# Layer-1 attention: row blocks' softmax sums inverted in pairs instead of one by one

## The chip, the cores and the metric

One Trainium2 chip, of which the program uses one core. The metric is the device time of one execution in microseconds, the median of three runs. TensorE is PE (its weight loads PEld), VectorE is DVE, ScalarE is ACT, GpSimd is POOL, and SyncE is SP.

## The reference, cut to what matters

Two layers. Each normalises `x`, and adds an attention and a feed-forward part to it. The change touches the attention of layer 1, a causal one with 32 query heads over 8 shared key/value heads of 128 elements, on 2 batches of 1024 rows with 512 features.

```python
# layer 1, attention
q = (hidden_states @ Wq.T)                     # 32 heads of 128
k, v = ...                                     # 8 heads of 128, through a low-rank latent
k = jnp.repeat(k, n_rep, axis=1)               # n_rep = 4
v = jnp.repeat(v, n_rep, axis=1)
scores = jnp.einsum('bhqd,bhkd->bhqk', q, k) * scale
scores = jnp.where(causal, scores, -1e9)
attn = jax.nn.softmax(scores, axis=-1)
out = jnp.einsum('bhqk,bhkd->bhqd', attn, v)
...
return out @ Wo.T
```

Layer 0 has a non-causal attention with one head of 128 and a branch with 50 Sinkhorn iterations; layer 1 also has a gated LoRA feed-forward (FFN).

## The kernel before

**Precision.** All matmuls work on float16. A float32 operand is held as a high part (its float16 rounding) and a low part (what is left, again in float16), and a product is made of three passes, high x high, high x low and low x high (`mm3`, L89).

**Row blocks.** Layer 1 runs over 16 groups (2 batches x 8 key/value heads, `g`), each with 32 row steps (`s`). A row step takes 32 query positions of the group's four heads, 128 rows in all, against the first W = 32(s+1) keys, since the attention is causal. It is traced by `row_step`, called at L868:

- `rows_scores`: the scores, by three matmuls into a PSUM bank of tag `s`, or six into two banks when W is over 512. There are four such banks (BS).
- `rows_exp`: on DVE, scale, mask and copy of the scores into `P`, with a running extremum into `nm` (L284 for the masked piece, L288 for the other); then on ACT `P = exp(P)` with the row's sum into `r[:, 0:1]` (L292).
- `rows_hi`: on DVE the reciprocal of the sum (L316), on ACT its scaling by 16384 (L317) and the high part of `P * r` into `Phl` (L322).
- `rows_lo`: on DVE the low part (L330; two pieces where a block's last key tile is mixed, in groups 8 to 15), on POOL a memset of the padding (L334), and on SP a DMA transpose of `Phl` into `PT` (L335).

`row_step` runs one step behind with the last two: step s traces the scores of block s, then `rows_hi` of block s-1, `rows_exp` of block s, and `rows_lo` of block s-1. The list `pending` holds at most one block.

**Buffers.** `P` has three buffers (PB) and `Phl` three (LB). A buffer holds four blocks for s below 8, two for s from 8 to 15, and one from 16 on (`share`). `nm` and `r` have four, `PT` three.

**Fillings.** After each row step of layer 1 come the pieces of other work that are due there (`fill`): the AV matmuls of a pair of blocks (`av`, L365), due in step 4c+2k+5 for blocks 4c+2k and 4c+2k+1, the evacuation of their result into `ao` (L105, L106), the output projection (`wo_block`, L755), the next group's query, key and value projections, the fetching of weights and their splitting on POOL (`parts_of`), and for part of the run the Sinkhorn iterations, the second layer norm, the gating and the FFN of the batches. Some of these are ordered behind the low part traced last (`last_low`).

**Order.** The order of tracing is a priority. The program is built with a planner (`schedule_with_timeline_sim=True`) that sets each engine's order of instructions by its own model of time, keeping dependencies, buffers and the orderings written out with `behind` and `issue_after`. So an engine's order in the profile differs from the order of tracing, and the score matmuls of two row steps often stand next to each other.

Layer 0 uses the same `row_step`, from L480, for 16 blocks of W = 1024, and flushes it with a `row_step()` without arguments (L483). Layer 1 does so once, after its last step.

Of the kernel before, what the change touches and what calls it, by code (L numbers as in the profile page):

```python
# [11 lines left out]
AF = mybir.ActivationFunctionType  # L12
# [4 lines left out]
P = 128  # L17
# [12 lines left out]
QR = 32  # L30
# [14 lines left out]
MG = range(8, 16)  # L45
# [3 lines left out]
PSCALE = 16384.0  # L49
# [3 lines left out]
def tile_model(ctx: ExitStack, tc: tile.TileContext, out: bass.AP, a: dict):  # L53
# [3 lines left out]
    V, A, G = nc.vector, nc.scalar, nc.gpsimd  # L57
# [7 lines left out]
    def T(tag, shape, dt=F32, bufs=None):  # L65
        count[0] += 1
        kw = {} if bufs is None else {"bufs": bufs}
        return sb.tile(shape, dt, tag=tag, name=f"{tag}_{count[0]}", **kw)
# [115 lines left out]
    last_hi, last_lo, last_low = [None], [None], [None]  # L184
# [82 lines left out]
    def share(got, n, k, make):  # L267

        if k % n == 0:
            got[0] = make()  # L270
        return got[0][:, k % n]

    P_of, hl_of = [None], [None]

    def rows_exp(pieces, causal, scale, n, k):

        W = pieces[-1][0] + pieces[-1][1]
        Pm = share(P_of, n, k, lambda: T("P", [P, n, S // n], bufs=PB))
        nm = T("nm", [P, 2], bufs=4)
        last = None  # L280
        for k, (o, w, pt) in enumerate(pieces):
            first = 1.0e30 if last is None else last
            if causal and o + w == W:
                last_row[0] = V.tensor_tensor_reduce(Pm[:, o:o + w], pt[:, :w], mask[:, 512 - w:],  # L284
                                       -scale, first, ALU.add, ALU.min,
                                       nm[:, k:k + 1])
            else:
                last_row[0] = V.tensor_scalar(Pm[:, o:o + w], pt[:, :w], -scale, first,  # L288
                                ALU.mult, ALU.min, accum_out=nm[:, k:k + 1])
            last = nm[:, k:k + 1]  # L290
        r = T("r", [P, 2], bufs=4)
        A.activation(Pm[:, :W], Pm[:, :W], AF.Exp, bias=last, scale=-1.0,  # L292
                     accum_out=r[:, 0:1])
        return Pm, r, W

    def rows_parts(W, n, k, mix=False):

# [14 lines left out]
        v = hl.rearrange("p (l k) -> p l k", l=2)  # L312
        return hl, v[:, 0, :W], [(0, W, v[:, 1, :W])], v[:, :, W:] if W < m * P else None

    def rows_hi(Pm, r, W, pool, hl):
        V.reciprocal(r[:, 1:2], r[:, 0:1])  # L316
        A.activation(r[:, 1:2], r[:, 1:2], AF.Copy, scale=PSCALE)  # L317
        if pool:
            A.activation(Pm[:, :W], Pm[:, :W], AF.Copy, scale=r[:, 1:2])
            A.activation(hl[1], Pm[:, :W], AF.Copy)  # L320
        else:
            A.activation(hl[1], Pm[:, :W], AF.Copy, scale=r[:, 1:2])  # L322

    def rows_lo(Pm, r, W, pool, hl, dst):
        whole, hi, los, pad = hl
        for a0, a1, lo in los:
            if pool:
                G.tensor_tensor(lo, Pm[:, a0:a1], hi[:, a0:a1], ALU.subtract)
            else:
                last_low[0] = V.scalar_tensor_tensor(lo, Pm[:, a0:a1], r[:, 1:2], hi[:, a0:a1],  # L330
                                                     ALU.mult, ALU.subtract)
        if pad is not None:

            behind(G.memset(pad, 0.0), last_low[0])  # L334
        nc.sync.dma_start_transpose(dst[:, :whole.shape[1] // P], whole)  # L335

    pending = []

    def row_step(q=None, K=None, W=None, causal=None, scale=None, dst=None, pool=None, n=1, k=0,
                 mix=False):  # L340

        if q is not None:
            pieces = rows_scores(q, K, W)
        old = None
        if pending:
            old = pending.pop()
            rows_hi(*old[:5])
        if q is not None:
            pending.append((*rows_exp(pieces, causal, scale, n, k), pool, rows_parts(W, n, k, mix), dst))
        if old:  # L350
            rows_lo(*old)

    def out_tile():
        count[0] += 1
# [311 lines left out]
    SC1 = 1.0 / (math.sqrt(128.0) * 128.0)  # L666
# [108 lines left out]
    def fetch_q(g, hh):  # L775
        qw[g, hh] = fetch(a["Wq"][4 * (g % NG) + hh])
# [8 lines left out]
    def layer1_attn(kv0, start, extra):  # L785


        N, NS = NB * NG, S // QR
        fill = {}

        def at(g, s, f):
            g, s = g + s // NS, s % NS
            fill.setdefault((g, s), []).append(f)

        kvs, Qs, PTs, avs, aos, wos = [{} for _ in range(6)]

        def twice(g):
            Vm = kvs[g]["Vm"] = [T("xr", [P, NT, P], F16, bufs=XB) for l in range(2)]
            for l in range(2):
                for k in range(2):  # L800
                    nc.sync.dma_start(Vm[l][64 * k:64 * k + 64], kvs[g]["V"][0:64, l])

        def q_unit(g, u):
            half, hh = divmod(u, 4)
            if hh == 0:
                Qs[g, half] = T("Q", [P, 2, NS // 2, 4, QR], F16, bufs=2)
            qproj(g // NG, qw[g, hh], Qs[g, half], hh, half)

        def fetch_wo(g, hh):
            n = 4 * (g % NG) + hh  # L810
            wos[g, hh] = fetch(a["WoT"][n * P:(n + 1) * P, :])

        def split_wo(g, hh):
            wos[g, hh] = parts_of(wos[g, hh], "wo", 32.0, WB)

        def av(g, c, k):
            if k == 0:
                avs[g, c] = out_tile()
            aos[g, c] = group_av(kvs[g]["V"], kvs[g].get("Vm"), PTs[g, 2 * c + k], c, k, avs[g, c])

        def wo(g, c):
            wo_block(g // NG, c, aos[g, c], [wos[g, h] for h in range(4)], g % NG == NG - 1)

        kvs[0], fs = kv0
        start(fs[2:], lambda u: q_unit(0, u))
        for hh in range(4):
            fetch_wo(0, hh)
            split_wo(0, hh)
        for g in range(N):
            if g + 1 < N:  # L830
                new = (g + 1) % NG == 0
                kvs[g + 1], fs = kv((g + 1) // NG, (g + 1) % NG)
                at(g, KVN - 2 if new else 1, fs[0])
                for k, f in enumerate(fs[1:]):
                    at(g, KVN + 2 * k if new else 1 + 4 * k + 2 * (k == 0), f)
                for hh in range(4):
                    at(g, 5 + 4 * hh, lambda g=g, hh=hh: fetch_q(g + 1, hh))
                    at(g, 7 + 4 * hh, lambda g=g, hh=hh: split_q(g + 1, hh))
                for u in range(4):
                    at(g, QNN + 2 * u if new else QN + 4 * u, lambda g=g, u=u: q_unit(g + 1, u))  # L840
                for hh in range(4):
                    s = 26 + 2 * hh if new else 22 + 3 * hh
                    at(g, s - 2, lambda g=g, hh=hh: fetch_wo(g + 1, hh))
                    at(g, s, lambda g=g, hh=hh: split_wo(g + 1, hh))
            for u in range(4):
                at(g, QH + (1 if (g + 1) % NG == 0 else 3) * u, lambda g=g, u=u: q_unit(g, 4 + u))
            if g in MG:
                at(g, 2, lambda g=g: twice(g))
            for c in range(NT):
                for k in range(2):  # L850
                    at(g, 4 * c + 2 * k + AVD, lambda g=g, c=c, k=k: av(g, c, k))
                at(g, 4 * c + WOD, lambda g=g, c=c: wo(g, c))
        for k, fs in extra.items():
            fill[k] = fs + fill.get(k, [])
        for g in range(N + 1):
            for s in range(NS):
                if g < N:
                    c, r = divmod(s, NR)

                    n = 4 if c < 2 else 2 if c < 4 else 1  # L860
                    if c < 4 and r == 0:
                        PT = T("PT", [P, 2 * (c + 1), NR, P], F16, bufs=3)
                        for k in range(2):
                            PTs[g, 2 * c + k] = PT[:, :, 2 * k:2 * k + 2]
                    elif c >= 4 and r % 2 == 0:
                        PTs[g, s // 2] = T("PT", [P, 2 * (c + 1), 2, P], F16, bufs=3)
                    Qt, q0 = Qs[g, s // (NS // 2)], s % (NS // 2)
                    row_step(lambda l: Qt[:, l, q0].rearrange("p h q -> p (h q)"),  # L868
                             kvs[g]["K"], QR * (s + 1), True, SC1, PTs[g, s // 2][:, :, r % 2], False, n, r, g in MG)
                elif pending:  # L870
                    row_step()
                for f in fill.pop((g, s), []):
                    f()
        assert not fill, sorted(fill)
# [131 lines left out]
    PTs = attn0_rows(0, 0, *f0[0][:2], lambda: adv(CA))  # L1006
    ys0 = branch0(0, *f0[0][3:5], lambda: adv(CB))
    attn0_out(0, 0, f0[0][2], PTs)
    PTs = attn0_rows(0, 1, *f0[0][:2], lambda: adv(CA))
# [6 lines left out]
    for half in range(2):  # L1016
# [5 lines left out]
        PTs = attn0_rows(1, half, *f0[1][:2], lambda: adv(CD))  # L1022
# [153 lines left out]
```

## Time and profile before

| | |
|---|---|
| median of 3 runs | 1848.31 us (1847.91 to 1849.43) |
| span of the profiled execution | 1846.2 us |
| PE busy, share of the span | 93% |
| DVE busy, share of the span | 80% |
| ACT busy, share of the span | 65% |
| L292 exponential, ACT, 528 of them | 391.5 us, mean 742 ns |
| L322 high part, ACT, 515 | 369.5 us, mean 730 ns |
| L330 low part, DVE, 627 | 460.8 us, mean 759 ns |
| L335 transpose, issue to landing, median | 3.2 us |

The span is the time from the first to the last instruction of one execution under the profiler. Busy time of an engine leaves out its waits. Matmuls are pipelined and their ends are modelled, so that a busy PE is not in itself a PE at its peak; the spacing of their starts tells more. Of a wait for several semaphores the last is named.

### The profile page before, as it was taken

How to read it: one execution, taken by the hardware profiler on the slowest of the kernel's cores; microseconds unless marked ns; L12 is line 12 of the kernel's file. 1: busy time of each engine (PE TensorE's matmuls, PEld its weight loads, DVE VectorE, ACT ScalarE, POOL GpSimd, SP SyncE). 2: the span in 40 equal slices, each digit the busy share in tenths (PEclk: the TensorE clock that was granted, in tenths of full speed). 3: DMA queues.
4: the chain of work that ended last, by engine and by line, in shares of the span. 5: the costliest groups of instructions: out<-in, count | busy, mean ns of one | idle time of the engine just before them, and what ended most of it. 6: DMA issues, size and time to landing. Idle time of an engine off the chain costs nothing.

```text
span 1846.2 us, 35059 instructions
## 1 busy us (share of the span) xinstructions
PE 1708.2 (93%) x11394; PEld 1038.5 (56%) x11394; DVE 1473.1 (80%) x4162; ACT 1191.1 (65%) x2917; POOL 896.5 (49%) x1476
## 2 busy tenths in 40 slices
PE   4666389999999999998999999999999999999998
PEld 2434146566666566655555566666666666666565
DVE  8888968988888878778976768778787877787675
ACT  4848666656676778876544656667666767676564
POOL 5568629778766465647634433323242424235200
PEclk9888699999999999999999999999999999999999
DMA  7435225656575656468645656556566655566455
GB/s 212 82 56 132 59 44 123 151 118 139 119 149 98 141 128 144 105 142 143 146 98 125 144 126 140 135 124 141 125 134 124 142 118 142 124 143 135 97 121 118
DMA packets 693482, 230.25 MB, mean 125 GB/s; under 512 B 674081, under 2 KB 674209, under 8 KB 693298
## 3 DMA queue, kind: packets, MB, share of 16 engines
q1 hardware_dynamic: 677842, 180.75, 47.3%
q0 software_dynamic: 13152, 43.07, 8.7%
q10 hardware_dynamic: 2304, 4.20, 0.7%
q8 instruction: 89, 1.46, 0.3%
q14 instruction: 95, 0.78, 0.1%
HBM read 52.81 MB, written 4.19 MB: 31 GB/s over the span
## 4 chain that ended last, share of the span: by engine, by line
PE 47%; DVE 2%; DMA 1%; POOL 1%; issue 1%; ACT 0%; SPq 0%; DVEq 0%
PE pp L89 26%; PE av L365 11%; PE s L89 10%; DVE Phl L330 0%; DVE f2k L913 0%; DMA f2k<-in_Wq 0%; DMA xT<-wo 0%; DVE P L288 0%; POOL wo L241 0%; DMA PT<-Phl 0%; POOL f2k L95 0%; SPq L335 0%; DVE P L284 0%; DMA twT<-twhl 0%; DVE Q L106 0%
## 5 line engine op out<-in xcount | busy, mean ns | idle before, releaser
L292 ACT ACTIVATE P<-P,nm 128x1024 f32<-128x1024 f32 (+31 forms) x528 | 391.5, 742 | 280.9 <-DVE nm L284 263.4
L330 DVE SCALAR_TENSOR_TENSOR Phl<-P,r,Phl 128x64 f16<-128x64 f32 (+16 forms) x627 | 460.8, 759 | 75.7 <-ACT Phl L322 70.3
L89 PE MATMUL s<-K,Q 128*128 128x512 f16 (+22 forms) x2400 | 439.1, 317 | 19.7 <-DVE P L288 11.7
L365 PE MATMUL av<-PT,V 128*128 128x256 f16 x3456 | 425.6, 274 | 9.4 <-DMA PT<-Phl 8.5
L365 PEld LDWEIGHTS <-V 128*128 128x128 f16 x3456 | 338.2, 98 | 92.9 <-DMA PT<-Phl 10.6
L322 ACT ACTIVATE Phl<-P,r 128x1024 f16<-128x1024 f32 (+31 forms) x515 | 369.5, 730 | 20.6 <-DMA PT<-Phl 5.3
L89 PE MATMUL pp<-xT,wq 128*128 128x512 f16 x1536 | 371.8, 381 | 4.5 <-DVE Q L106 2.3
L89 PE MATMUL pp<-wo,ao 128*128 128x512 f16 x1536 | 369.9, 379 | 2.0 <-ACT ao L105 1.9
L95 POOL TENSOR_SCALAR f2k<-f2k 128x512 f32<-128x512 f32 x164 | 113.9, 695 | 500.6 <-DVE Phl L330 458.9
L89 PEld LDWEIGHTS <-Q 128*128 128x128 f16 x2400 | 222.8, 98 | 175.7 <-issue 27.7
L89 PEld LDWEIGHTS <-wq 128*128 128x128 f16 x1536 | 149.7, 98 | 172.6 <-issue 6.8
L89 PEld LDWEIGHTS <-ao 128*128 128x128 f16 x1536 | 149.5, 98 | 156.9 <-ACT ao L105 3.4
L284 DVE CUSTOM_DVE_ANT_0 P<-s,mask,nm 128x272 f32<-128x272 f32 (+15 forms) x256 | 157.3, 615 | 9.3 <-PE s L89 1.0
L288 DVE TENSOR_SCALAR_CACHE_REDUCE P<-s 128x512 f32<-128x512 f32 (+15 forms) x272 | 152.6, 562 | 13.4 <-PE s L89 11.2
L316 DVE RECIPROCAL r<-r 128x1 f32<-128x1 f32 x528 | 78.9, 154 | 87.5 <-ACT P L292 84.5
L317 ACT ACTIVATE r<-r 128x1 f32<-128x1 f32 x528 | 95.6, 192 | 60.2 <-DVE r L316 59.7
L105 ACT ACTIVATE ao<-av 128x512 f16<-128x512 f32 x128 | 74.9, 585 | 81.7 <-PE av L365 81.5
L334 POOL MEMSET Phl<- 128x192 f16 (+1 forms) x320 | 56.2, 189 | 142.3 <-DMA PT<-Phl 97.3
L105 ACT ACTIVATE Q<-pp 128x512 f16<-128x512 f32 x128 | 74.6, 583 | 64.3 <-PE pp L89 60.0
L284 DVE CUSTOM_DVE_ANT_0 P<-s,mask 128x32 f32<-128x32 f32 (+15 forms) x256 | 103.7, 430 | 14.9 <-PE s L89 14.2
L755 DVE SCALAR_TENSOR_TENSOR acc<-pp,acc 128x512 f32<-128x512 f32 x128 | 87.1, 681 | 35.1 <-PE pp L89 34.7
L106 DVE SCALAR_TENSOR_TENSOR Q<-pp,Q 128x512 f16<-128x512 f32 x128 | 87.4, 683 | 34.0 <-ACT Q L105 33.7
(256 smaller groups left out, 2153.1 us busy)
## 6 DMA issues: line engine op xcount, KB each, us to landing
f2k<-in_Wq POOLq DMA_DIRECT2D x64, 256.0 KB, 3.1
f2k<-in_WoT POOLq DMA_DIRECT2D x64, 256.0 KB, 3.3
PT<-Phl SPq DMA_TRANSPOSE x528, 3.2
acc<-in_x SPq DMA_DIRECT2D x16, 256.0 KB, 5.1
f2k<-in_Wup POOLq DMA_DIRECT2D x16, 256.0 KB, 3.3
out<-acc ACTq DMA_DIRECT2D x16, 256.0 KB, 3.5
xr<-V SPq DMA_DIRECT2D x32, 128.0 KB, 2.4
xr<-in_x SPq DMA_DIRECT2D x12, 256.0 KB, 3.9
```

The lines of the kernel that those rows point to most:

```text
L89: nc.tensor.matmul(dst, lhs(l), rhs(r), start=(i == 0 and j == 0), stop=(i == n - 1 and j == 2))
L95: first = G.tensor_scalar(stage, stage, scale, 1.0, ALU.mult, ALU.mult)
L105: A.activation(hl_hi, src, AF.Copy, scale=scale)
L106: return V.scalar_tensor_tensor(hl_lo, src, scale, hl_hi, ALU.mult, ALU.subtract)
L284: last_row[0] = V.tensor_tensor_reduce(Pm[:, o:o + w], pt[:, :w], mask[:, 512 - w:], -scale, first, ALU.add, ALU.min, nm[:, k:k + 1])
L288: last_row[0] = V.tensor_scalar(Pm[:, o:o + w], pt[:, :w], -scale, first, ALU.mult, ALU.min, accum_out=nm[:, k:k + 1])
L292: A.activation(Pm[:, :W], Pm[:, :W], AF.Exp, bias=last, scale=-1.0, accum_out=r[:, 0:1])
L317: A.activation(r[:, 1:2], r[:, 1:2], AF.Copy, scale=PSCALE)
L322: A.activation(hl[1], Pm[:, :W], AF.Copy, scale=r[:, 1:2])
L330: last_low[0] = V.scalar_tensor_tensor(lo, Pm[:, a0:a1], r[:, 1:2], hi[:, a0:a1], ALU.mult, ALU.subtract)
L365: nc.tensor.matmul(p, v, pt, start=(k == 0), stop=(k == len(todo) - 1))
L755: V.scalar_tensor_tensor(acc[b, t], p, 1.0 / 256.0, acc[b, t], ALU.mult, ALU.add)
```

## The change

In layer 1 a tile `r` holds the sums of two row blocks and their inverses, four columns in place of two. The even block's exponential opens it and writes its sum to column 0, the odd block's writes to column 1. `pending` gathers blocks until both are there. The next even row step then makes one reciprocal and one scaling for both (`rows_inverse`), the high parts of both blocks before its own exponential, and the low parts, memsets and transposes of both after it. An odd row step traces only its scores and its exponential. Layer 0 keeps one block at a time (`rows=1`), with the same instructions as before.

```diff
--- before.py
+++ after.py
@@ -272,7 +272,7 @@
 
     P_of, hl_of = [None], [None]
 
-    def rows_exp(pieces, causal, scale, n, k):
+    def rows_exp(pieces, causal, scale, n, k, total):
 
         W = pieces[-1][0] + pieces[-1][1]
         Pm = share(P_of, n, k, lambda: T("P", [P, n, S // n], bufs=PB))
@@ -288,10 +288,9 @@
                 last_row[0] = V.tensor_scalar(Pm[:, o:o + w], pt[:, :w], -scale, first,
                                 ALU.mult, ALU.min, accum_out=nm[:, k:k + 1])
             last = nm[:, k:k + 1]
-        r = T("r", [P, 2], bufs=4)
         A.activation(Pm[:, :W], Pm[:, :W], AF.Exp, bias=last, scale=-1.0,
-                     accum_out=r[:, 0:1])
-        return Pm, r, W
+                     accum_out=total)
+        return Pm, W
 
     def rows_parts(W, n, k, mix=False):
 
@@ -312,43 +311,52 @@
         v = hl.rearrange("p (l k) -> p l k", l=2)
         return hl, v[:, 0, :W], [(0, W, v[:, 1, :W])], v[:, :, W:] if W < m * P else None
 
-    def rows_hi(Pm, r, W, pool, hl):
-        V.reciprocal(r[:, 1:2], r[:, 0:1])
-        A.activation(r[:, 1:2], r[:, 1:2], AF.Copy, scale=PSCALE)
+    def rows_inverse(r):
+        n = r.shape[1] // 2
+        V.reciprocal(r[:, n:], r[:, :n])
+        A.activation(r[:, n:], r[:, n:], AF.Copy, scale=PSCALE)
+
+    def rows_hi(Pm, W, inv, pool, hl):
         if pool:
-            A.activation(Pm[:, :W], Pm[:, :W], AF.Copy, scale=r[:, 1:2])
+            A.activation(Pm[:, :W], Pm[:, :W], AF.Copy, scale=inv)
             A.activation(hl[1], Pm[:, :W], AF.Copy)
         else:
-            A.activation(hl[1], Pm[:, :W], AF.Copy, scale=r[:, 1:2])
-
-    def rows_lo(Pm, r, W, pool, hl, dst):
+            A.activation(hl[1], Pm[:, :W], AF.Copy, scale=inv)
+
+    def rows_lo(Pm, W, inv, pool, hl, dst):
         whole, hi, los, pad = hl
         for a0, a1, lo in los:
             if pool:
                 G.tensor_tensor(lo, Pm[:, a0:a1], hi[:, a0:a1], ALU.subtract)
             else:
-                last_low[0] = V.scalar_tensor_tensor(lo, Pm[:, a0:a1], r[:, 1:2], hi[:, a0:a1],
+                last_low[0] = V.scalar_tensor_tensor(lo, Pm[:, a0:a1], inv, hi[:, a0:a1],
                                                      ALU.mult, ALU.subtract)
         if pad is not None:
 
             behind(G.memset(pad, 0.0), last_low[0])
         nc.sync.dma_start_transpose(dst[:, :whole.shape[1] // P], whole)
 
-    pending = []
+    pending, sums = [], [None]
 
     def row_step(q=None, K=None, W=None, causal=None, scale=None, dst=None, pool=None, n=1, k=0,
-                 mix=False):
+                 mix=False, rows=1):
 
         if q is not None:
             pieces = rows_scores(q, K, W)
-        old = None
-        if pending:
-            old = pending.pop()
-            rows_hi(*old[:5])
+        old = []
+        if pending and (q is None or len(pending) == pending[0][1].shape[1] // 2):
+            old, pending[:] = pending[:], []
+            rows_inverse(old[0][1])
+            for o in old:
+                rows_hi(*o[0][:5])
         if q is not None:
-            pending.append((*rows_exp(pieces, causal, scale, n, k), pool, rows_parts(W, n, k, mix), dst))
-        if old:
-            rows_lo(*old)
+            if not pending:
+                sums[0] = T("r", [P, 2 * rows], bufs=4)
+            r, i = sums[0], len(pending)
+            Pm, w = rows_exp(pieces, causal, scale, n, k, r[:, i:i + 1])
+            pending.append(((Pm, w, r[:, rows + i:rows + i + 1], pool, rows_parts(W, n, k, mix), dst), r))
+        for o in old:
+            rows_lo(*o[0])
 
     def out_tile():
         count[0] += 1
@@ -866,7 +874,7 @@
                         PTs[g, s // 2] = T("PT", [P, 2 * (c + 1), 2, P], F16, bufs=3)
                     Qt, q0 = Qs[g, s // (NS // 2)], s % (NS // 2)
                     row_step(lambda l: Qt[:, l, q0].rearrange("p h q -> p (h q)"),
-                             kvs[g]["K"], QR * (s + 1), True, SC1, PTs[g, s // 2][:, :, r % 2], False, n, r, g in MG)
+                             kvs[g]["K"], QR * (s + 1), True, SC1, PTs[g, s // 2][:, :, r % 2], False, n, r, g in MG, 2)
                 elif pending:
                     row_step()
                 for f in fill.pop((g, s), []):
```

## The prediction

> **What bounds the kernel now.** I read the page first (part 1), then the busy time by stretch, then what TensorE waited for in each stretch.
>
> ```profile
> span 1846.2 us, 35059 instructions
> PE 1708.2 (93%) x11394; PEld 1038.5 (56%) x11394; DVE 1473.1 (80%) x4162; ACT 1191.1 (65%) x2917; POOL 896.5 (49%) x1476
> ```
> ```profile
> 265.00:640.00 375.00, 369.06 (x2541) 228.61 (x2541) 319.12 (x925) 250.35 (x622) 264.14 (x545) 1.00 0.59 125
> 640.00:1016.00 376.00, 358.11 (x2412) 217.32 (x2409) 296.07 (x796) 251.27 (x666) 209.55 (x301) 0.99 0.62 131
> 1016.00:1800.00 784.00, 782.73 (x5168) 479.46 (x5169) 608.33 (x1695) 511.05 (x1235) 262.70 (x443) 1.00 0.59 130
> ```
>
> The second fence has, after the stretch and its length, PE, PEld, DVE, ACT and POOL busy, then granted clock and DMA. Layer 1 runs from about 265 us on. From 1016 to 1800 PE is busy 782.73 of 784 us at clock 1.00, and this is not only the modelled ends: the 512-column matmuls of that stretch start 216 ns apart almost without exception, the 256-column ones 109 ns, so that each follows the last at once. In this half of the kernel no cheaper row step can bring anything, since PE waits for none. What can be won lies before: 5.9 us of idle PE from 265 to 640, 17.9 us from 640 to 1016. Their causes, for the second stretch:
>
> ```profile
> PE av L365 <- DMA PT<-Phl: 4.0, 3, 2.2
> PE s L89 <- DVE nm L284: 3.6, 3, 1.6
> PE pp L89 <- DVE acc L755: 2.2, 1, 2.2
> PE pp L89 <- DVE Q L106: 1.9, 1, 1.9
> PE s L89 <- DVE P L288: 1.7, 1, 1.7
> ```
>
> A DVE that is late costs here 9.4 us in these four rows, 11.2 with two small ones of gating (1.1 and 0.7). From 265 to 640 the same view gives 6.1 us in four rows. So **17.3 us** is the most that a faster DVE can return, and 4.0 more hang on the transposes.
>
> **The change, part by part.**
>
> *Removed.* 512 row blocks of layer 1 make 256 pairs: 256 reciprocals and 256 scalings go.
>
> ```profile
> L316 DVE RECIPROCAL r<-r 128x1 f32<-128x1 f32 x528 | 78.9, 154 | 87.5 <-ACT P L292 84.5
> L317 ACT ACTIVATE r<-r 128x1 f32<-128x1 f32 x528 | 95.6, 192 | 60.2 <-DVE r L316 59.7
> ```
>
> DVE: 256 x 0.154 = 39.4 us of busy time; ACT: 256 x 0.192 = 49.2 us. The 256 that stay are two elements wide. No such form is in the trace; it lies between the 128x1 row (154 ns) and the reciprocal of Sinkhorn at L564 (128x32, median 352 ns), that is about 6 ns an element: I take +6 ns, 1.6 us in all; the upper end, 198 ns each, would take the DVE gain away and add 11 us of busy time. On ACT, 128x8 takes 196 to 203 ns against 192: +2 ns, nothing. DVE also stood idle 84.5 us before the 528 reciprocals, waiting for the sums; with the even blocks' reciprocals gone, up to half of that, 42 us, goes too. None of this is on PE's path after 1016. Before it, DVE is relieved by some 20 us (8.2 groups x 16 pairs x 0.154) of its 615 busy in 751 us, 3%. It can return nothing, or all of 17.3; those waits are single late evacuations and maxima of 1 to 2 us, which a relief of 0.15 us a pair shortens and does not remove. I take **-2 us**.
>
> [...]
>
> *Moved.* The even block's high part (L322), low part (L330), memset (L334) and transpose (L335) now follow the exponential of the odd block. How late that is can be read in the trace:
>
> ```profile
> 1221.07 0.79 ACT L292 ACTIVATE P<-P,nm 128x608 f32<-128x608 f32 x1
> 1222.99 0.79 ACT L322 ACTIVATE Phl<-P,r 128x608 f16<-128x608 f32 x1
> 1223.81 0.85 DVE L330 SCALAR_TENSOR_TENSOR Phl<-P,r,Phl 128x608 f16<-128x608 f32 x1
> ...
> 1228.39 0.83 ACT L292 ACTIVATE P<-P,nm 128x640 f32<-128x640 f32 x1 [4.61 <-DVE nm L284]
> 1229.13 0.19 ACT L292 ACTIVATION_READ_ACCUMULATOR P<-P,nm 128x1 f32 x1
> ...
> 1231.63 0.52 DVE L288 TENSOR_SCALAR_CACHE_REDUCE P<-s 128x352 f32<-128x352 f32 x1
> ```
>
> Columns: start, duration, instruction. The even block of width 608 got its high part at 1222.99; its partner's sum is read out at 1229.32, and with 0.16 and 0.2 us for the joint inverse and some 0.13 of hand-overs the high part can start at 1229.81: 6.8 us later. I did this for all 256 pairs: in 139 the even high part already starts after the odd exponential, because the planner runs two row steps side by side, and nothing moves; in the other 117 the shift is 4.0 us on average. Who waits for a late even block:
>
> - **Its P buffer.** For widths over 512 (steps 16 to 31) a block has a P tile of its own, and there are three (PB). The maximum of block e+3 writes the buffer of block e and so waits for its low part. In the fence that is the last row, width 704, at 1231.63; the low part would end at about 1231.5, just in time. Over the 111 such pairs I could match, shift minus the distance from the low part's end to that maximum is positive in 37, 45.8 us together. Behind that maximum on DVE stand the evacuations, and PE waits at the score matmuls of block e+5, which reuse the four score banks; they follow the maximum by 3.0 us at the median, so only 4 of the 37 reach PE, with **+4.2 us**. Lower end 0 (the planner orders around it), upper end 45.8 (nothing is hidden).
> - **The AV matmuls.** They come three steps after the pair's flush, as before. The odd block, the later one, now stands behind the even block's high and low parts, at most about 1.2 us. From its transpose's issue plus 3.2 us (the page's median to landing) to PE's first use the distance is 2.3 us or more in 95 of 100 pairs, 6.6 at the median. No pair is late by this sum: 0. Without that cover a pair would cost up to 1.2 us.
> - **Queues.** Two transposes come on SP back to back (median 1.3 us each); behind them stand the FFN's transpose (L987), for which PE waited 0.2 us after 1016, and the copies of L801. On ACT an evacuation (L105) can stand behind two high parts instead of one, up to 1.15 us; three pp banks hide it. POOL's splits wait for the last low part traced: an earlier one in odd steps, one up to 1.3 us later in even steps; PE hardly waits for them (0.8 us). 0 for all three; uncovered, 1.2 us at a time.
>
> *The end.* The last two blocks are flushed together:
>
> ```profile
> 1828.74 1.29 DVE L330 SCALAR_TENSOR_TENSOR Phl<-P,r,Phl 128x1024 f16<-128x1024 f32 x1 [0.53 <-ACT Phl L322]
> ...
> 1835.85 2.78 PE L365 MATMUL av<-PT,V 128*128 128x256 f16 x24
> ```
>
> The last low part ends at 1830.03 and now ends 1.2 us later; plus 3.2 for the landing that is 1834.4, and PE comes to it at 1835.85: 0, at worst +1.2.
>
> **The sum**, against the profiled execution: 1846.2 - 2 + 4.2 = 1848.4. The median of the runs shown, 1848.31, is 2.1 above that span, so **1850.5 us** is forecast, +0.1%. A difference under 0.2% (3.7 us) I count as no change, which is about what a measurement of this kernel can tell. The likeliest case alone spans 1845 to 1852.
>
> **Rivals.**
>
> *Slower: the three P buffers become the bound of the wide steps.* The cycle is low(e), low(e+1), maximum(e+3), its exponential, inverse, scaling, high: at width about 1000, 1.25 + 1.29 + 1.58 + 1.21 + 0.15 + 0.2 + 1.12 = 6.8 us plus hand-overs, about 7.0, against 7.3 us that PE takes for two steps near the end (1799.1 to 1813.7 for four). At the middle widths 6.2 to 6.4 against 6.7. For it: the margin is 0.3 us, and an evacuation of 0.68 us on DVE in the wrong place uses it up. Against: score banks and 22% free DVE time smooth it. It decides where the pair's cycle passes PE's time for two steps. A quarter of the 45.8 us through to PE gives 1848.3 - 2 + 11.5, about 1858; half 1869.
>
> *Faster: DVE relief.* If half of 17.3 us comes back and the P waits stay hidden: 1848.3 - 8.6, about 1840. For it: DVE is busiest (88% of 900 to 950) just where PE idles. Against: the same stretch has the longest shifts.
>
> *The planner's order.* All engines' orders are made anew from a model of time, so idle PE before 1016 can move by some us either way without any of these causes. It has no price of its own; it widens the range.
>
> **How the numbers follow.** Forecast (within 0.2%) 0.38; slower by the P buffers or a worse order 0.36; faster 0.26. The range takes 1840 from the faster case and 1864 from between a quarter and half of the P lateness; about one in ten is left on each side.
>
> **What would show it.** Reciprocals of r fall from 528 to 272, DVE busy by about 38 us, ACT by 49. Right: PE still over 99% busy from 1016 to 1800 and its idle time before 1016 near 24 us. The P rival: PE waits for L284 or L288 after 1016, where there are none now. The faster case: the DVE rows of the third fence shrink by half. Wrong altogether: new waits of PE for PT.

## The result, and the profile after

The changed kernel takes **1874.54 us** (median of four runs, 1873.62 to 1875.73) against 1848.84 of the kernel before: ratio 1.0134, 95% interval 1.012 to 1.0149. It is slower by 25.7 us, and the forecast of no change missed it. The profiled execution spans 1871.9 us.

The page of the changed kernel, parts 1 and 5 (lines have moved by a few: L291 is the exponential, L324 the high part, L332 the low part, L373 the AV matmul):

```profile
span 1871.9 us, 34615 instructions
PE 1718.4 (92%) x11394; PEld 1039.1 (56%) x11394; DVE 1427.5 (76%) x3906; ACT 1154.9 (62%) x2661; POOL 856.8 (46%) x1476
...
L324 ACT ACTIVATE Phl<-P,r 128x1024 f16<-128x1024 f32 (+31 forms) x515 | 350.6, 729 | 27.8 <-DMA PT<-Phl 17.5
...
L316 DVE RECIPROCAL r<-r 128x2 f32<-128x2 f32 (+1 forms) x272 | 43.3, 159 | 88.7 <-ACT P L291 87.2
```

ACT now waits 17.5 us, not 5.3, for Phl buffers that are still being transposed (L324). The change did what it says: 272 reciprocals in place of 528, which are busy 43.3 us in place of 78.9, and scalings busy 51.3 us in place of 95.6. All in all DVE is busy 45.6 us less, ACT 36.2 us. The time went up all the same. By stretch (length, then busy time of PE, PEld, DVE, ACT, POOL, then clock and DMA):

```profile
265.00:640.00 375.00, 366.86 (x2517) 226.37 (x2515) 307.21 (x853) 236.44 (x552) 246.20 (x543) 1.00 0.59 124
640.00:1016.00 376.00, 355.91 (x2412) 215.77 (x2411) 287.16 (x730) 244.31 (x605) 192.16 (x296) 0.99 0.61 128
1016.00:1800.00 784.00, 770.28 (x5051) 468.27 (x5049) 568.73 (x1532) 483.39 (x1090) 258.01 (x448) 1.00 0.61 129
```

In the last stretch PE was busy 782.73 of 784 us before and is now busy 770.28; it also starts 117 matmuls fewer in it. What it waits for there:

```profile
PE pp L89 <- ACT ao L105: 4.3, 5, 1.6
PE av L373 <- DMA PT<-Phl: 4.2, 5, 2.8
PE pp L89 <- DMA xT<-wo: 2.7, 1, 2.7
PE s L89 <- DVE P L288: 2.1, 4, 0.5
```

Before, the first, second and fourth of these rows were not there at all. Waits of PE for PT and for L288 are what the prediction had named as signs of being wrong and of its slower rival. What the three rows have in common is the row blocks' chain: a transpose that lands late, an evacuation that stands on ACT behind high parts, a maximum that comes late on DVE. The longest wait of the second row (2.8 us) and the third row belong to the time before 1040 us, still in group 7. An evacuation behind high parts looks like this, in group 9:

```profile
1210.43 1.09 ACT L324 ACTIVATE Phl<-P,r 128x352 f16<-128x352 f32 x2 [1.21 <-DMA PT<-Phl]
...
1211.43 0.57 ACT L105 ACTIVATE ao<-av 128x512 f16<-128x512 f32 x1
...
1212.06 0.60 PE L89 MATMUL pp<-wo,ao 128*128 128x512 f16 x2 [1.60 <-ACT ao L105]
```

**Lost time, the measure of what follows.** The program's work for PE is the same in every variant (11394 matmuls). So I add up, from each matmul's start to the next one's, what exceeds its columns at 2.4 columns a nanosecond. That rate is the trace's own: from 1016 to 1800 us of the kernel before, matmuls of 512 columns start 216 ns apart and those of 256 start 109 ns apart, so that 256 more take 107, or 2.4 columns a nanosecond (the expectation of e5 writes it as 2.4 GHz). What is left over by it, 2.7 ns at 512 columns and 2.3 at 256, alone adds up to 1.5 us in a group: 1.5 is a group in which PE never waits, and 10.5 the floor of groups 8 to 14. By stretch:

| lost PE time, us | layer 0 | groups 0-7 | groups 8-14 | group 15 and end | all |
|---|---|---|---|---|---|
| before | 108.4 | 52.2 | 10.8 | 4.5 | 175.9 |
| changed | 110.0 | 62.8 | 21.5 | 7.7 | 202.0 |
| difference | 1.6 | 10.6 | 10.7 | 3.2 | 26.1 |

The 26.1 us are the whole difference of the spans (25.7). They are two losses: 10.6 us in the crowded groups 0 to 7 (Sinkhorn, layer norm, gating, the change of batch), and 13.9 in the plain groups from 8 on, where PE had not waited at all before the end. In groups 8 to 14, up to the first scores of group 15, it is 15 waits of 0.3 to 1.8 us, 10.2 us together, and each of them lies in the first 32 us of a group, which takes about 92: four of 0.7 us among its first score matmuls, then waits at AV and for evacuations. The wide steps themselves go without a wait. The four hang on the maximum of the last block of the group before, which writes the P buffer of the block of width 928 and comes behind the low parts of a whole pair, as here:

```profile
1189.17 2.57 DVE L332 SCALAR_TENSOR_TENSOR Phl<-P,r,Phl 128x896 f16<-128x896 f32 x4 [1.40 <-ACT Phl L324]
...
1191.66 0.69 DVE L288 TENSOR_SCALAR_CACHE_REDUCE P<-s 128x512 f32<-128x512 f32 x1
...
1192.41 0.29 PE L89 MATMUL s<-K,Q 128*128 128x96 f16 x3 [0.53 <-DVE P L288]
```

The end of the changed kernel shows the second loss at work (timeline: start, duration, instruction, idle time before it and its releaser):

```profile
1839.65 1.07 ACT L291 ACTIVATE P<-P,nm 128x928 f32<-128x928 f32 x1 [0.48 <-DVE nm L284]
...
1840.63 0.19 ACT L291 ACTIVATION_READ_ACCUMULATOR P<-P,nm 128x1 f32 x1
...
1843.38 1.09 ACT L291 ACTIVATE P<-P,nm 128x960 f32<-128x960 f32 x1 [2.56 <-DVE nm L284]
...
1843.87 0.81 PE L89 MATMUL s<-K,Q 128*128 128x512 f16 x3
...
1844.47 1.11 ACT L291 ACTIVATE P<-P,nm 128x992 f32<-128x992 f32 x1
...
1844.60 0.17 DVE L316 RECIPROCAL r<-r 128x2 f32<-128x2 f32 x1 [0.19 <-ACT P L291]
...
1845.58 0.19 ACT L317 ACTIVATE r<-r 128x2 f32<-128x2 f32 x1
1845.80 2.05 ACT L324 ACTIVATE Phl<-P,r 128x928 f16<-128x928 f32 x2
...
1846.90 2.57 DVE L332 SCALAR_TENSOR_TENSOR Phl<-P,r,Phl 128x896 f16<-128x896 f32 x4 [2.14 <-ACT Phl L324]
...
1849.39 0.68 DVE L288 TENSOR_SCALAR_CACHE_REDUCE P<-s 128x512 f32<-128x512 f32 x1
...
1851.45 1.15 ACT L291 ACTIVATE P<-P,nm 128x1024 f32<-128x1024 f32 x1 [3.59 <-DVE nm L284]
...
1854.52 2.45 DVE L332 SCALAR_TENSOR_TENSOR Phl<-P,r,Phl 128x992 f16<-128x992 f32 x2 [0.55 <-ACT Phl L324]
...
1855.12 2.47 PE L373 MATMUL av<-PT,V 128*128 128x256 f16 x21 [1.22 <-DMA PT<-Phl]
...
1861.50 2.79 PE L373 MATMUL av<-PT,V 128*128 128x256 f16 x24 [1.54 <-DMA PT<-Phl]
```

Width 928 is an even block. Its sum is read out at 1840.82, but its high part starts at 1845.80, since the joint inverse waits for the exponential of width 960, which starts at 1843.38, and its scaling then stands on ACT behind the exponential of width 992. DVE stands idle for 2.14 us until the first high part is there, does both blocks' low parts in a row (2.57 us), and only then, at 1849.39, the maximum of the last block. The first half of that block's scores stood ready since 1844.68; but it writes the P buffer that the block of width 928 held, three blocks earlier. In the kernel before, the same scores started at 1822.79 and their maximum at 1824.07:

```profile
1822.79 1.46 PE L89 MATMUL s<-K,Q 128*128 128x512 f16 x6
...
1824.07 0.67 DVE L288 TENSOR_SCALAR_CACHE_REDUCE P<-s 128x512 f32<-128x512 f32 x1
```

So the last exponential is late, and the last two blocks are flushed late and together. PE waits 1.22 us for the transposes of the pair of widths 928 and 960, and 1.54 us for those of the last pair.

### The profile page after: what moved, and what is told of

It is laid out like the page before. It is cut to its first block, busy times and chain, and to the rows that moved or that the text cites. A ratio compares the mean times of both kernels' runs of the same rounds, so it can differ in the third digit from the quotient of the medians.

```text
span 1871.9 us, 34615 instructions
## 1 busy us (share of the span) xinstructions
PE 1718.4 (92%) x11394; PEld 1039.1 (56%) x11394; DVE 1427.5 (76%) x3906; ACT 1154.9 (62%) x2661; POOL 856.8 (46%) x1476
## 5 line engine op out<-in xcount | busy, mean ns | idle before, releaser
L291 ACT ACTIVATE P<-P,nm 128x1024 f32<-128x1024 f32 (+31 forms) x528 | 391.2, 741 | 370.7 <-DVE nm L284 353.9
L332 DVE SCALAR_TENSOR_TENSOR Phl<-P,r,Phl 128x64 f16<-128x64 f32 (+16 forms) x627 | 430.8, 726 | 113.4 <-ACT Phl L324 110.1
L89 PE MATMUL s<-K,Q 128*128 128x512 f16 (+22 forms) x2400 | 444.3, 318 | 25.3 <-DVE P L288 14.1
L373 PE MATMUL av<-PT,V 128*128 128x256 f16 x3456 | 427.1, 275 | 15.8 <-DMA PT<-Phl 11.7
L373 PEld LDWEIGHTS <-V 128*128 128x128 f16 x3456 | 337.3, 99 | 102.9 <-DMA PT<-Phl 13.4
L89 PE MATMUL pp<-wo,ao 128*128 128x512 f16 x1536 | 373.8, 380 | 12.1 <-ACT ao L105 11.5
L324 ACT ACTIVATE Phl<-P,r 128x1024 f16<-128x1024 f32 (+31 forms) x515 | 350.6, 729 | 27.8 <-DMA PT<-Phl 17.5
L95 POOL TENSOR_SCALAR f2k<-f2k 128x512 f32<-128x512 f32 x164 | 104.0, 635 | 528.3 <-DVE Phl L332 483.4
L288 DVE TENSOR_SCALAR_CACHE_REDUCE P<-s 128x512 f32<-128x512 f32 (+15 forms) x272 | 152.4, 563 | 19.7 <-PE s L89 17.5
L105 ACT ACTIVATE ao<-av 128x512 f16<-128x512 f32 x128 | 75.0, 586 | 102.6 <-PE av L373 99.7
L284 DVE CUSTOM_DVE_ANT_0 P<-s,mask 128x32 f32<-128x32 f32 (+15 forms) x256 | 104.5, 432 | 14.3 <-PE s L89 13.4
L316 DVE RECIPROCAL r<-r 128x2 f32<-128x2 f32 (+1 forms) x272 | 43.3, 159 | 88.7 <-ACT P L291 87.2
L89 PEld LDWEIGHTS <-xT 128*128 128x128 f16 x864 | 63.4, 102 | 75.1 <-DMA xT<-wo 44.4
L89 PE MATMUL pp<-cmp,xT 128*128 128x128 f16 (+2 forms) x720 | 86.0, 273 | 17.2 <-DMA xT<-wo 15.7
```

Of the source, the lines that this page charges most:

```text
L89: nc.tensor.matmul(dst, lhs(l), rhs(r), start=(i == 0 and j == 0), stop=(i == n - 1 and j == 2))
L95: first = G.tensor_scalar(stage, stage, scale, 1.0, ALU.mult, ALU.mult)
L105: A.activation(hl_hi, src, AF.Copy, scale=scale)
L324: A.activation(hl[1], Pm[:, :W], AF.Copy, scale=inv)
L332: last_low[0] = V.scalar_tensor_tensor(lo, Pm[:, a0:a1], inv, hi[:, a0:a1], ALU.mult, ALU.subtract)
L373: nc.tensor.matmul(p, v, pt, start=(k == 0), stop=(k == len(todo) - 1))
```

## The experiments

My theory after the result: **the binding** of the even block to the odd one's sum makes a chain (maximum, exponential, inverse, high, two low parts, next maximum) that PE feels, by way of the three P buffers and of late transposes. The rivals: the burst of moved work as such; the Phl buffers and the transposes; the removed instructions; and **the planner's order**, which is made anew for every program and was good for the kernel before. The kernel before was timed beside the variants each time and spread more there (1843.8 to 1860.3 us) than at first, so the ratios are to be read, and where there is only one timed run, the lost time by stretch.

**e1, the move alone.** Each block has its own inverse again; the tracing order of the change stays.

```diff
-            rows_inverse(old[0][1])
-            for o in old:
+            for i, o in enumerate(old):
+                V.reciprocal(o[0][2], o[1][:, i:i + 1])
+                A.activation(o[0][2], o[0][2], AF.Copy, scale=PSCALE)
                 rows_hi(*o[0][:5])
```

> The changed kernel, but each block of a pair has a reciprocal and a scaling of its own again (528 of each); the order of tracing, with both blocks' parts in the next even row step, stays. If the loss comes from moving the even blocks' parts (theory: burst of two blocks' high parts, low parts and transposes), the time stays where the changed kernel is, 1870 to 1882 us. If the joint, wider inverse itself costs, it returns towards 1849.

1859.85 us, ratio 1.0044 (1.0024 to 1.0064): between the two kernels, and neither of the two times expected. Lost time 106.2, 63.4, 10.8, 4.5. The move costs nothing from group 8 on: tracing order is only a priority, and with an inverse of its own the even block's parts go ahead when they can. From the read-out of an even block's sum to the end of its low part it takes 3.33 us before (median, groups 8 to 15), 3.55 in e1, and 6.04 with the change. Here is the stretch from 1200 to 1700 us, well inside the plain groups, for before, changed, and e1 (first number after the length is PE):

```profile
1200.00:1700.00 500.00, 500.00 (x3329) 309.11 (x3327) 395.50 (x1109) 334.59 (x807) 174.92 (x295) 1.00 0.60 131
```
```profile
1200.00:1700.00 500.00, 493.32 (x3275) 303.00 (x3274) 370.53 (x1015) 318.26 (x725) 167.11 (x290) 1.00 0.63 130
```
```profile
1200.00:1700.00 500.00, 500.00 (x3325) 308.69 (x3323) 386.75 (x1114) 334.54 (x817) 163.38 (x286) 1.00 0.61 130
```

Before and e1 have PE busy in all of the 500 us, the changed kernel in 493.32.

**e2, the saving alone.** In the kernel before, layer 1's even blocks skip the reciprocal and the scaling and use the bare sum as their factor.

```diff
+        inv = r[:, -1:]
+        if r.shape[1] == 2:
-        V.reciprocal(r[:, 1:2], r[:, 0:1])
-        A.activation(r[:, 1:2], r[:, 1:2], AF.Copy, scale=PSCALE)
+            V.reciprocal(inv, r[:, 0:1])
+            A.activation(inv, inv, AF.Copy, scale=PSCALE)
...
-        return Pm, r, W
+        return Pm, r[:, 0:1] if bare else r, W
```

> The kernel before, without the reciprocal and scaling of layer 1's even blocks, which use the bare sum in the inverse's place (those rows of the attention are scaled wrongly); nothing is moved. If saving these instructions is harmless and only the move costs, 1842 to 1851 us. If any change of the instruction mix makes the planner find a worse order (rival: planner's noise), 1855 us or more.

1864.43 us, ratio 1.0062 (1.0042 to 1.0082). Lost time 107.6, 69.8, 11.7, 5.2.

```profile
1200.00:1700.00 500.00, 500.00 (x3338) 309.98 (x3336) 382.26 (x1019) 323.66 (x730) 166.39 (x289) 1.00 0.61 130
```

DVE is relieved (382.26 us against 395.50) and PE has nothing of it, because it was busy throughout. And taking work away makes groups 0 to 7 *slower* by 17.6 us. A longer queue is not to be expected from fewer instructions; an order made anew can do it, though no run shows the order by itself as the cause.

**e3 and e4, later AV.** The changed kernel, and the kernel before as a control, with

```diff
-AVD, WOD = 5, 10
+AVD, WOD = 6, 11
```

(`AVD` is the 5 in the due step of the AV matmuls, 4c+2k+5; `WOD` is the corresponding number of the output projection.)

> The changed kernel with the AV matmuls and the output projection due one row step later (AVD 6, WOD 11). If PE waits because the pair's transposes land late, this gives them 2 to 3 us more and half of the 26 us or more comes back: 1862 us or less. If the loss is in the buffers of P or Phl, which a later AV does not free, the time stays at 1870 us or above.

> The kernel before with AVD 6 and WOD 11, the control for the run with the same setting: it also shows how much a mere shift of due times, which saves and moves nothing in the row steps, does. Expected within 5 us of 1849 if the planner's order is robust; 1860 or more if the order is so finely tuned that any shift costs as much as the change did.

e3: 1863.80 us, 1.0063 (1.0047 to 1.0078), lost 109.4, 61.6, 16.8, 4.3, between the two figures expected. Late transposes are a part: the loss at the end is gone, that of groups 8 to 14 nearly halved, not gone. e4: 1860.24 us, 1.0042 (1.0022 to 1.0063), lost 106.6, 62.1, 10.8, 4.6. This control saves nothing and moves nothing in the row steps, and loses 9.9 us in groups 0 to 7, as much as the change. Its time lies outside the 5 us that I expected of a robust order, at the edge of the 1860 of a fine-tuned one.

**e5 to e8, a fourth buffer of P or Phl.** The room for a fourth buffer is taken from two other kinds of tile, f2k and xr, with three buffers each in place of four. That changes layer 0 too (121 us lost instead of 108), so the base (e5) and the kernel before (e8) ran with these as well.

```diff
-FB, PB, LB, XB, WB = 4, 3, 3, 4, 9
+FB, PB, LB, XB, WB = 3, 3, 3, 3, 9   # e5, e8
+FB, PB, LB, XB, WB = 3, 4, 3, 3, 9   # e6
+FB, PB, LB, XB, WB = 3, 3, 4, 3, 9   # e7
```

> The changed kernel with three f2k buffers and three xr buffers in place of four and four, which makes room for a fourth P or Phl: the base for the next two. PE's lost time (start to start of matmuls, less their columns at 2.4 GHz) in groups 8 to 14 was 10.5 us before, 21.5 with the change, 10.6 with the move alone. Expected here: still 17 us or more there, if weights fetched into fewer buffers don't matter; the whole 1872 to 1890 us.

> The same with four P buffers. If the maximum of block e+3 waiting for the even block's low part is what costs in the steady groups (theory P), PE's lost time in groups 8 to 14 falls to 10 to 13 us; if the Phl buffers and the transposes cost (theory Phl) or the late AV (theory AV), it stays within 3 us of the base.

> The same with four Phl buffers and three of P. If high parts wait on ACT for transposes that come in bursts, and evacuations behind them (theory Phl), lost time in groups 8 to 14 falls to 10 to 13 us; by theory P it stays within 3 us of the base.

> The kernel before with three f2k and three xr buffers: the control. Lost time in groups 8 to 14 10 to 12 us if these buffers don't matter in the steady groups; before group 8 it may be up to 10 us worse than before's 52 us, as every other variant so far is (61.6 to 69.8 us).

| one run each | us | groups 0-7 | groups 8-14 | group 15 and end |
|---|---|---|---|---|
| e5 changed, small | 1869.74 | 52.9 | 13.7 | 8.3 |
| e6 changed, P 4 | 1868.65 | 55.2 | 11.6 | 8.4 |
| e7 changed, Phl 4 | 1871.90 | 51.3 | 18.4 | 8.5 |
| e8 before, small | 1867.81 | 60.8 | 10.8 | 4.2 |

Four P buffers bring groups 8 to 14 to the floor:

```profile
1200.00:1700.00 500.00, 500.00 (x3336) 309.88 (x3335) 373.49 (x1021) 322.56 (x730) 168.17 (x293) 1.00 0.61 132
```

In a quarter of the wide pairs of e6 the maximum of block e+3 starts 1.29 us or more before the even block's low part ends, which three buffers forbid (groups 8 to 15); in the changed kernel the maximum starts 1.34 us after that end at the median, against 3.14 before the change. A fourth Phl buffer does not help: e7 loses 4.7 us more than the base, outside the 3 expected. But the base itself had only 13.7 us, below the 17 expected (and its time is below the 1872), so that these single runs alone do not decide between P and a luckier order. Neither buffer mends the end. And with small buffers the *changed* kernel loses less in groups 0 to 7 than the unchanged one (52.9 against 60.8), which speaks against laying the 10.6 us there to the binding.

**e9, the inverse done twice.** `for _ in old: rows_inverse(old[0][1])` in place of one call.

> The changed kernel with its joint reciprocal and joint scaling done twice over for each pair: 528 of each again, as before, but both blocks' parts still wait for the odd block's sum. Against the move alone (10.8 us of lost PE time in groups 8 to 14, 4.5 in group 15 and the end) it adds only the binding. If the binding of the even block to the odd one costs in the steady groups: 17 us or more in groups 8 to 14 and 7 or more in group 15. If instead the saved instructions are what upsets the order: 10 to 12 and 4 to 5 us.

1925.53 us, ratio 1.0396 (1.0351 to 1.0442), lost 110.0, 99.6, 30.2, 13.4. I had meant it to restore the count of instructions only, but the second reciprocal overwrites what the first scaling wrote, so it waits for it, and the figures expected (both of them passed) decide nothing. The reciprocals' own releasers show

```profile
  ACT P L291: 90.5, 114
  ACT r L317: 45.0, 83
```

where the second row is new. So this kernel measures something else: a longer chain. Two instructions of 0.16 and 0.2 us and their hand-overs make about 0.45 us a pair; with the queues, the way from the odd block's sum to the even block's high part grows from 1.43 to 2.39 us at the median (groups 8 to 15). That costs 51 us over the changed kernel, 36.8 of them in groups 0 to 7 and 14.4 from group 8 on. The time that PE loses follows the length of the pair's chain.

**e10, two P buffers in the kernel before** (`PB` 2).

> The kernel before with two P buffers in place of three; nothing bound, nothing saved. The maximum of block b then waits for the low part of block b-2, about as tight as block e+3 behind a low part that comes one step late. Theory P: lost time in groups 8 to 14 rises from 10.8 us to 17 or more. Theory Phl or AV: it stays at 10.8 to 12.

1876.04 us in one run. Of the 28 us that it loses more, half is in layer 0, which has two buffers as well (122.6 us lost there). Groups 8 to 14 lose 14.0 us, not 17: a miss. A tight P without the binding costs about 3 us there, where the changed kernel with three buffers loses 10.7 more than before.

**e11, four P buffers and the later AV** (e6 with AVD 6, WOD 11).

> The changed kernel with four P buffers (three f2k, three xr) and AVD 6, WOD 11. If P buffers cost in the steady groups and late transposes at the end, both are mended: 10.8 to 12 us in groups 8 to 14 and 4 to 5 in group 15 and the end, where four P buffers alone left 8.4.

1859.05 us in one run; lost 116.4, 54.7, 10.8, 4.2. Both losses of the plain groups are gone:

```profile
1200.00:1700.00 500.00, 500.00 (x3331) 309.27 (x3329) 371.53 (x1023) 324.75 (x727) 161.46 (x289) 1.00 0.59 129
```

It is still no gain over the kernel before: there is nothing below the floor, and the small buffers cost 8 us in layer 0.

**e12, a second shift without content.** The kernel before with `WOD` 11 alone.

> The kernel before with only the output projection due one row step later (WOD 11, AVD 5): a second shift that touches no row step. Theory of the planner's order: groups 0 to 7 lose 58 us or more against 52.2 before (the other five variants with four f2k buffers lost 61.6 to 69.7), groups 8 to 14 stay at 10.8; in all 1.002 to 1.006 of before. If before's order is nothing special, 50 to 55 us in groups 0 to 7 and a ratio within 0.2% of 1.

1861.49 us, 1.0056 (1.0036 to 1.0076); groups 0 to 7 lose 60.3 us, as expected. Groups 8 to 14 lost 18.9, not 10.8, but 6.6 of the excess lie in one group, behind one single wait:

```profile
PE av L365 <- DMA PT<-Phl: 4.1, 1, 4.1
```

**e13, binding with the old count of instructions.** A second reciprocal and scaling for each pair, into a spare tile that nothing reads, off the chain.

```diff
             rows_inverse(old[0][1])
+            spare, m = T("spare", [P, 2], bufs=2), len(old)
+            V.reciprocal(spare[:, :m], old[0][1][:, :m])
+            A.activation(spare[:, :m], spare[:, :m], AF.Copy, scale=PSCALE)
```

> The changed kernel with a second reciprocal and scaling for each pair into a spare tile that nothing reads: 528 of each as before, the chain from sums to high parts no longer than in the changed kernel. If the binding costs in the steady groups, lost PE time in groups 8 to 14 is 16 us or more and in group 15 with the end 7 or more, and the whole 1.01 or more of before. If the saved instructions upset the order, 10 to 12 and 4 to 5 us, as in the move alone.

1880.12 us, 1.0156 (1.0123 to 1.0188), lost 108.3, 71.6, 20.6, 7.9. In groups 8 to 15 that is the changed kernel again, so the saved instructions are not what costs there:

```profile
1200.00:1700.00 500.00, 493.84 (x3274) 303.44 (x3272) 377.62 (x1110) 328.22 (x827) 163.99 (x289) 1.00 0.62 130
```

**e14, e9's longer chain with four P buffers and the later AV.**

> The doubled inverse of e9 with four P buffers (three f2k, three xr) and AVD 6, WOD 11. In e9 the chain, longer by about 0.45 us a pair, took the lost time from 202.0 to 253.2 us. If the chain costs because of the three P buffers and the early AV, lost time here is at most 15 us above e11's 186.1. If it costs in another way (ACT or DVE queues, Phl), 30 us or more above.

1877.65 us in one run, lost 120.5, 64.0, 15.6, 4.2: 204.3 in all, 18.2 above e11, where the same lengthening had cost 51.2 with three. It falls between the two figures: P buffers and AV carry about two thirds of what a longer chain costs, not all.

## Why the prediction was wrong

*What bounds the kernel* was right: PE, without a wait after 1016 us, so that a cheaper row step has nothing to bring there. e2 shows it: 500.00 of 500 us busy with and without the saving.

*Removed instructions*: right in size. Taken were 39.4 us of DVE and 6 ns more for the wider form; measured are 78.9 - 43.3 = 35.6 and 5 ns. The -2 us of relief before 1016 was not seen. e2, the relief alone, came out slower, so that whatever relief there is, the new order hides it.

*The even block's P buffer*, +4.2 us between 0 and 45.8: **this is the step that failed.** I shifted each even block by itself, subtracted PE's slack of 3.0 us at the score banks, and found that "only 4 of the 37 reach PE". The lateness does not end there: a late maximum makes its own exponential late, that exponential holds the next joint inverse, and the next even block is later still. The traces show it gathering. From the start of a block's last score matmul to the start of its exponential (medians of groups 8 to 15), the kernel before takes 1.4 to 2.0 us at widths 576 to 800 and the changed one 1.2 to 2.3; at width 960 it is 2.6 before, 5.6 in the changed kernel and 7.0 in e9, but 2.4 in e1 and 1.6 in e11. So the wide blocks fall behind towards the end of a group, and PE meets it in the first steps of the next one. The rival named this cycle with its figures (about 7.0 against 7.3 us for two steps, 6.2 to 6.4 against 6.7), a margin of 0.3 us, and I let the slack at one point outweigh it. Together with AV, the queues and the end it cost 13.9 us (10.7 + 3.2): four runs without the binding do not have it (e1, e2, e4, e8), the runs with binding and three P buffers have it in some degree (changed, e3, e5, e7, e9, e13), and four P buffers with a later AV take it away (e11). One run without the binding, e12, loses 8.1 us more than the kernel before in groups 8 to 14, most of it behind one wait; so a loss of this size there can come about in another way too.

*AV matmuls*, 0: the distance to the landing was large in the median, but the shift of the odd block, "at most about 1.2 us", was taken from an unchanged odd block. Its own path also grew: from its sum to the end of its low part 3.54 us before, 4.38 after. PE now waits for PT, and e3 shows that a step more of time mends a part.

*The end*, 0, at worst +1.2: 3.2 with group 15. The last two blocks are not only flushed one behind the other; their exponential was late already, as the timeline shows.

*Queues*, 0, since "three pp banks hide it": this failed too, as the last link of the chain. From 1200 to 1700 us PE waited 6.3 us, and 4.3 of them for evacuations (L105), as in the lines of group 9 above. With four P buffers there are none in that stretch (e6), with four Phl buffers there are (e7), so that by these single runs the burst behind which they stand comes from P.

*The planner's order*, "no price of its own": it has one, about 10 us, the other half of the miss. Of the variants with four f2k buffers and a chain no longer than the change's, all seven lost 60 to 72 us in groups 0 to 7 where the kernel before loses 52.2: the move, the saving, the spare inverse, the change with a later AV, the two P buffers, and two shifts of due times that have nothing to do with row blocks. But with three f2k buffers the changed kernel loses 51 to 55 us there (e5, e6, e7, e11) and the unchanged one 60.8 (e8): the order can fall out well or badly, with the binding and without it. The longer chains of e9 and e14 lose more than the kernels they lengthen in these groups too (99.6 and 64.0 us), so the binding may have a part in the 10.6. That they are the planner's order, and not some cause common to all seven, is argued from these runs; no run held the old order fixed under the change.

Against the forecast span the miss is 23.5 us. By lost time it is 9.7 of the binding (13.9 less the 4.2 forecast), 10.6 in groups 0 to 7, 2 of relief that did not come, and 1.6 in layer 0: 23.9 us, as the lost time grew by 0.4 more than the span.

## What to carry to other kernels

Joining two small instructions ties two chains together at the later one. Count the wait, not the instruction: 0.35 us saved a pair was paid with 2.7 us of delay for the even block, and with a chain whose pace was, by the prediction's own figures, within a few per cent of PE's. When lateness can feed on itself through a ring of buffers, work out the cycle of the ring; the slack at one consumer does not tell. And before an effect under 1% is given to a change in a kernel with a planned order, run a change without content beside it: here that cost 0.4 to 0.6%.

## What the runs showed that I had not expected

After a wait of 4.13 us in e12 PE ran at half speed: of the 24 AV matmuls of 256 columns behind it, 15 in a row, from 0.8 us after the restart on, start 213 ns apart in place of 109, and the granted clock of that stretch is 0.91:

```profile
1380.00:1400.00 20.00, 15.87 (x89) 9.21 (x87) 10.37 (x28) 7.14 (x21) 5.10 (x10) 0.91 0.47 57
```

The 15 matmuls take 3.2 us (15 x 213 ns), so that the stall of 4.13 us cost 5.7 us with the 1.6 us they lost (15 x 104 ns). The same is seen after a shorter wait: earlier in the same run PE waited 3.00 us, until 1022.83, and then ran for a time at a granted clock of 0.66 in the mean:

```profile
1023.00:1028.00 5.00, 5.00 (x20) 2.34 (x19) 1.23 (x1) 1.21 (x2) 4.13 (x7) 0.66 0.72 182
```

This bears on groups 0 to 7, where the granted clock fell to 0.50 four times in the kernel before, for 3.4 us each (from 359.8, 844.5, 861.6 and 936.7 us), and five times in the changed one (from 467.7, 751.0, 870.5 and 928.5 for 3.4 us, from 1024.1 for 6.8). The matmuls that ran so lost about 6.5 us there in the kernel before, 8.6 in the changed one and 12.8 in e2; so some 2 of the 10.6 us and 6 of the 17.6 come from the clock and not from the waits themselves.
